# Layer 0's attention scores from float32 to three float32r passes, with the positions on four column tiles and the FFN's sign weights in DRAM

## The chip, the cores and the metric

The kernel runs on one core of a Trainium2 chip. The metric is the device time of one launch in microseconds (us). Kernels are timed in rounds beside the kernel before on the same chip, and nearly all executions agree within 0.3%. A ratio in this text is the mean time of one kernel's fast runs over that of the other's fast runs of the same rounds, so it is not quite the ratio of the medians that stand beside it. The granted clock is the share of its full clock that PE, the engine for matrix products, was given in a stretch.

## The reference

Eight images of 32 x 32 positions with 384 channels go through two layers. Cut to what matters here:

```python
# layer 0 (after a group norm): 6 heads of 64, T = 1024 positions, decomposed relative positions
attn = einsum('bqd,bkd->bqk', q * SCALE, k)
attn = attn + rel_h[:, :, :, :, None] + rel_w[:, :, :, None, :]   # rel_h = q . Rh, rel_w = q . Rw
out  = softmax(attn) @ v;  x = x + (out @ proj_w + proj_b)
# layer 1: causal attention with one head of 384; then, for images 0 to 4 only, an FFN with sign weights
y = quantize(gelu(quantize(ln(x) @ sign(W1 - mean) + b1)) @ sign(W2 - mean) + b2)
```

The scores of layer 0 are by far the largest product: 8 images x 6 heads x 1024 x 1024.

## The kernel before

PE, DVE, ACT and POOL are the engines for matrix products, vector work, activations and general work (GpSimd). SBUF is the memory on the chip that they work on, PSUM the one that PE writes its products to. Column tiles are narrow weights (64 or 32 columns) that stand side by side in PE. Layer 0 handles two heads (a pair `p`, with `par` 0 and 1) at a time. Queries and keys carry the positions in the same 128 rows: 64 rows of q or k, and 64 rows of positions (in `qa`) or of unit rows (in `ka`), so that one float32 product gives q.k plus both position terms.

```python
# POOL: unit rows of ka, 12 copies of 32x1024 for each image                      (L377)
unit = ident[r, r].unsqueeze(2 - d).to_broadcast([32, H, W])
nc.gpsimd.tensor_copy(ka[par][r, p, :].rearrange("i (h w) -> i h w", h=H), unit)
...
# positions: 16 PSUM tiles for each image, 8 small matmuls each, two column tiles  (L402, L403)
nc.tensor.matmul(ps[r0 : r0 + 32, ts(i, 96)], rel[src, 0, win], qv[:, :, at, :], start=True, stop=True)
nc.tensor.matmul(ps[r0 + 32 : r0 + 64, ts(i, 96)], rel[src, 1, win], qv[:, :, :, at], start=True, stop=True)
...   # one DVE copy (L406) and one ACT copy (L409) of each tile into qa
# scores: two float32 matmuls for a 128 x 1024 tile, from a ring of two PSUM tiles (L423, L427)
for half in range(2):
    nc.tensor.matmul(sc[:, half, :], ka[par][:, p, ts(c, P)], qa[par][:, p, ts(half, 512)], start=True, stop=True)
nc.scalar.activation(pr, sc.rearrange("p a n -> p (a n)"), AF.Exp)
...
# P.V: the two heads on two column tiles of 64                                     (L439)
nc.tensor.matmul(avs[half][ts(par, HD), :], v[:, c, ts(h, HD)], prs[par][:, ts(half, 512)], ...)
```

A step `c` of a pair makes the scores of two tiles, then P.V of the step before. There are 3 pairs x 8 steps x 8 images = 192 steps. The order of instructions on each engine is decided when the program is built.

## Time and profile before

| | kernel before |
|---|---|
| time, median | 2955.96 us |
| PE busy | 94% |
| largest group | scores of layer 0, 704 us |
| step of layer 0's attention | 5.50 us |
| prologue (q, k, v, positions) after an FFN / without | 52.8 / 61.0 us |

The profile is read from the bound inwards: the sums say that PE is the bound, the groups say which of its work is largest and that this work waits for nothing, and the timeline gives durations of a stage. The lines themselves are in the prediction below.

### The profile page before, as it was taken

What the parts mean: (1) busy time and instruction counts of PE and PEld (TensorE: products, weight loads), DVE (VectorE), ACT (ScalarE), POOL (GpSimd) and SP (SyncE); (2) the same over time, 40 slices, a digit from 0 to 9 for tenths busy, and PEclk for the clock granted to TensorE, in tenths of its full rate; (3) what the DMA queues carried; (4) which work ended last, traced back from release to release, by engine and by line L of the source; (5) the groups of instructions that cost most, each with busy time, mean ns of one, the idle gap of its engine ahead of it and who ended that gap; (6) DMA issues with size and microseconds to landing.
All of it is one profiled execution on the core that took longest, in us unless ns stands there. A gap on an engine that the chain in (4) does not pass through costs nothing.

```text
span 2952.4 us, 26382 instructions
## 1 busy us (share of the span) xinstructions
PE 2782.4 (94%) x10692; PEld 1460.8 (49%) x10692; DVE 1457.6 (49%) x2402; ACT 929.0 (31%) x1170; POOL 165.4 (6%) x139
## 2 busy tenths in 40 slices
PE   6996989999999999999998999999998999899998
PEld 3433567335664345753457633567434553455345
DVE  3457366453473544744536555357355245523452
ACT  1431154331354312533215432134431143113320
POOL 3000010000020000100001000011001000100000
PEclk9997999999999999999999999999999999999999
DMA  3001001000010000010000100001000100010000
GB/s 108 22 0 64 1 1 65 0 0 1 0 65 1 1 1 0 1 65 0 1 0 1 65 0 1 0 0 65 1 1 0 65 1 0 1 43 1 0 1 23
DMA packets 28066, 49.04 MB, mean 17 GB/s; under 512 B 4256, under 2 KB 24096, under 8 KB 27936
## 3 DMA queue, kind: packets, MB, share of 16 engines
q1 hardware_dynamic: 23648, 43.65, 4.1%
q10 hardware_dynamic: 4288, 3.61, 0.4%
q8 instruction: 86, 1.41, 0.2%
q14 instruction: 44, 0.36, 0.0%
HBM read 34.68 MB, written 12.58 MB: 16 GB/s over the span
## 4 chain that ended last, share of the span: by engine, by line
PE 55%; issue 35%; DVE 5%; ACT 3%; DMA 1%; POOL 0%; ACTq 0%; POOLq 0%; DVEq 0%
PE f_s L423 20%; PE f_av L439 10%; PE f_y L671 6%; PE f_v L329 5%; PE f_qk L319 4%; ACT f_qa L409 3%; PE f_av L569 2%; PE f_s L555 2%; DVE f_h L657 2%; PE f_q L319 2%; PE f_pj L329 1%; PE f_den L451 1%; DVE f_x L680 1%; DVE f_y L679 1%; DMA bv<-in_qkv_b 0%
## 5 line engine op out<-in xcount | busy, mean ns | idle before, releaser
L423 PE MATMUL f_s<-f_qa,f_ka 128*128 128x512 f32 x1536 | 703.9, 603 | 8.3 <-ACT f_qa L409 8.3
L427 ACT ACTIVATE f_pr<-f_s 128x1024 f32<-128x1024 f32 x384 | 393.3, 1024 | 651.4 <-PE f_s L423 651.3
L435 DVE TENSOR_TENSOR f_sum<-f_sum,f_pr 128x1024 f32<-128x1024 f32 x288 | 351.2, 1224 | 344.9 <-ACT f_pr L427 344.3
L423 PEld LDWEIGHTS f_s<-f_qa,f_ka 128*128 128x128 f32 x1536 | 277.9, 189 | 428.0 <-issue 311.2
L439 PE MATMUL f_av<-f_pr,f_v 128*64 128x512 f32 x1536 | 366.6, 603 | 0.0
L319 PE MATMUL f_qk<-f_gnT,wqkv_sb 128*128 128x512 f32 x576 | 254.0, 596 | 2.1 <-DVE f_gnT L278 1.1
L439 PEld LDWEIGHTS f_av<-f_pr,f_v 128*64 128x64 f32 x1536 | 94.3, 136 | 253.5 <-issue 222.6
L671 PE MATMUL f_y<-w2s,f_lo 128*128 128x384 f32 x480 | 172.1, 359 | 34.1 <-DVE f_lo L660 34.1
L569 PE MATMUL f_av<-f_v,f_pr 128*128 128x385 f32 x576 | 194.5, 486 | 0.0
L555 PE MATMUL f_s<-f_q,f_lnT 128*128 128x512 f32 (+3 forms) x576 | 193.8, 486 | 0.0
L319 PEld LDWEIGHTS f_qk<-f_gnT,wqkv_sb 128*128 128x128 f32 x576 | 109.3, 191 | 131.7 <-issue 125.4
L671 PE MATMUL f_y<-w2s,f_hi 128*128 128x384 f32 x480 | 169.5, 353 | 2.7 <-ACT f_hi L658 2.7
L569 PEld LDWEIGHTS f_av<-f_v,f_pr 128*128 128x128 f32 x576 | 108.6, 190 | 78.6 <-issue 11.5
L555 PEld LDWEIGHTS f_s<-f_q,f_lnT 128*128 128x128 f32 x576 | 103.1, 190 | 83.0 <-issue 57.4
L329 PE MATMUL f_pj<-wproj_sb,f_oT 128*128 128x384 f32 x384 | 129.8, 495 | 10.7 <-DVE f_oT L462 10.5
L409 ACT COPY f_qa<-f_rel 32x384 f32<-32x384 f32 x128 | 103.0, 804 | 117.0 <-DVE f_qa L406 114.1
L319 PE MATMUL f_q<-f_lnT,wqk 128*128 128x512 f32 x288 | 136.3, 624 | 0.0
L329 PE MATMUL f_v<-wv_sb,f_lnT 128*128 128x384 f32 x384 | 126.5, 486 | 0.0
L329 PE MATMUL f_v<-wqkv_sb,f_gnT 128*128 128x384 f32 x384 | 126.0, 486 | 0.0
L640 PE MATMUL f_y<-f_lnT,w1s 128*128 128x512 f32 x360 | 118.5, 406 | 5.7 <-ACT f_lnT L301 3.4
L646 DVE TENSOR_REDUCE am<-f_h 128x1 f32<-128x1024 f32 x60 | 73.2, 1220 | 102.0 <-ACT f_h L645 102.0
L454 DVE STREAM_TRANSPOSE f_tr<-f_den 128x512 f32<-128x512 f32 x48 | 34.4, 717 | 168.6 <-PE f_den L451 165.9
(130 smaller groups left out, 2981.9 us busy)
## 6 DMA issues: line engine op xcount, KB each, us to landing
f_gnT<-in_xT SPq DMA_DIRECT2D x24, 512.0 KB, 7.8
f_x<-in_x SPq DMA_DIRECT2D x32, 384.0 KB, 5.1
out_y<-f_x SPq DMA_DIRECT2D x32, 384.0 KB, 2.5
wqkv_sb<-in_qkv_w ACTq DMA_DIRECT2D x1, 1728.0 KB, 10.4
f_w_w<-in_w1T SPq DMA_DIRECT2D x1, 1536.0 KB, 6.2
f_w_w<-in_w2T SPq DMA_DIRECT2D x1, 1536.0 KB, 8.1
f_w_w<-in_w1T SPq DMA_DIRECT2D x1, 768.0 KB, 4.4
f_w_w<-in_w2T SPq DMA_DIRECT2D x1, 768.0 KB, 8.9
```

The lines of the kernel that those rows point to most:

```text
L319: nc.tensor.matmul(ps[:, half, :], w[:, k, cols], xT[:, k, ts(half, 512)], start=(k == 0), stop=(k == NC - 1),)
L329: nc.tensor.matmul(ps[:, :C], xT[:, k, ts(j, P)], w[:, k, cols], start=(k == 0), stop=(k == NC - 1))
L409: nc.scalar.copy(qa[par][rw, :, :].rearrange("k p (h w) -> k p w h", h=H)[:, :, 4 * g : 4 * g + 4, :], pv[rw])
L423: nc.tensor.matmul(sc[:, half, :], ka[par][:, p, ts(c, P)], qa[par][:, p, ts(half, 512)], start=True, stop=True)
L427: nc.scalar.activation(pr, sc.rearrange("p a n -> p (a n)"), AF.Exp)
L435: nc.vector.tensor_tensor(sums[par], prev, prs[par], ALU.add)
L439: nc.tensor.matmul(avs[half][ts(par, HD), :], v[:, c, ts(h, HD)], prs[par][:, ts(half, 512)], start=(c == 0), stop=(c == NJ - 1),)
L555: nc.tensor.matmul(sc[:, half, lo:], xT[:, k, ts(c, P)], q[:, k, half * 512 + lo : (half + 1) * 512], start=(k == 0), stop=(k == NC - 1),)
L569: nc.tensor.matmul(av[:, : C + 1], prs[c][:, ts(j - c, P)], v[:, c, :], start=(c == 0), stop=(c == j))
L640: nc.tensor.matmul(ps[:, half, :], w1s[:, i // 2, ts(m, P)], xs[i % 2][:, i // 2, ts(half, 512)], start=(i == 0), stop=(i == n - 1),)
L646: nc.vector.tensor_reduce(am[:, m : m + 1], h, AX.X, ALU.max, apply_absolute_value=True)
L671: nc.tensor.matmul(ps[:, :C], hs[i][:, m, :], w2s[:, half * 6 + m, :], start=(half == m == i == 0), stop=(half == i == 1 and m == 5),)
```

## The change

The intent is to make the scores cheaper. In the traces a float32 matmul of 512 columns takes two records, about 0.9 us, and a float32r one a single record, 0.2315 us. Each value is split into hi (the value in float32r) and lo (what is left of it). Three float32r products then stand for the float32 one: k(hi,lo) with q(hi,lo) gives two of the terms, the swapped `ks` with q the cross terms, and unit rows with the positions' hi and lo the rest. Everything else follows from that: q must be split before the positions are made, `ks` is copied by POOL, the positions get their own tile `r` with hi and lo, and to make room in SBUF the FFN's sign weights move to DRAM and are loaded for each image with an FFN.

```diff
+            def hi_lo(dst, hi, lo, ps, bias):
+                nc.scalar.activation(dst[hi], ps[hi], AF.Identity, bias=bias[hi])
+                nc.vector.scalar_tensor_tensor(dst[lo], ps[hi], bias[hi], dst[hi].bitcast(F32), ALU.add, ALU.subtract)
 ...
+            def positions(g):        # 4 PSUM tiles for each image, from the scores' ring, four column tiles
+                ps = pools.s_tile(f"rel_{b}_{g}")...
+                            nc.tensor.matmul(ps[ts(2 * par + d, 32), i, :96], rel[:, d, win], ..., start=True, stop=True)
+                for par in range(2):
+                    for d in range(2):
+                        nc.scalar.copy(dst[ts(hi, 32)], src)                                     # L418
+                        nc.vector.tensor_tensor(dst[ts(lo, 32)], src, dst[ts(hi, 32)].bitcast(F32), ALU.subtract)  # L419
 ...
+            for m in range(NPAIR): queries_keys(m)             # q
+            for g in range(4): positions(g)
+            for m in range(NPAIR, 2 * NPAIR): queries_keys(m)  # k, and its swapped copy ks on POOL
+            (v)
 ...
-                for half in range(2):
-                    nc.tensor.matmul(sc[:, half, :], ka[par][:, p, ts(c, P)], qa[par][:, p, ts(half, 512)], start=True, stop=True)
+                for i, (keys, queries) in enumerate(sides[p][par]):     # (k, q), (ks, q), (unit, r)
+                    for half in range(2):
+                        nc.tensor.matmul(sc[:, half, :], keys[:, ts(c, P)], queries[:, ts(half, 512)], start=(i == 0), stop=(i == 2))
 ...
-    w1s = const.tile([P, NC, FF], F32R, name="w1s")
+    w1s = store.tile([P, NC * FF], F32R, name="w1s")            # DRAM; loaded for each FFN by sign_weights(b)
```

The 12 copies of unit rows on POOL for each image are gone with `ka`.

More of the change, by code (lines that the diff above doesn't have):

```diff
@@ L44, in pool @@
             return ctx.enter_context(tc.tile_pool(name=f"{path}_{name}", bufs=bufs, **kw))
-        self.x = pool("x", 1)
-        self.image_ = pool("image", 8)
-        self.page_ = pool("page", 8 if self.fast else 7)
+        self.image_ = pool("image", 11)
+        self.page_ = pool("page", 10 if self.fast else 8)
         self.work = pool("work", 2)
@@ L98, in load_x @@
     def load_x(pools, b):
-        t = pools.x.tile([P, NJ, C], F32, tag="x", name=f"{pools.path}_x_{b}")
+        t = pools.flat(f"x_{b}")[:, : NJ * C].rearrange("p (j c) -> p j c", j=NJ)
         src = x[b].rearrange("(j p) c -> p j c", p=P)
@@ L158, in conv_attn_hybrid @@
     qscale = HD**-0.5
-    bq = const.tile([P, NPAIR], F32, name="bq")
-    nc.vector.tensor_scalar_mul(bq, bqk[:, 0:NPAIR], qscale)
+    nc.vector.tensor_scalar_mul(bqk[:, 0:NPAIR], bqk[:, 0:NPAIR], qscale)
     nc.vector.tensor_scalar_mul(rel, rel, 1.0 / qscale)
+    for k in range(NC):
+        nc.vector.tensor_scalar_mul(wqkv_sb[:, k, 0:C], wqkv_sb[:, k, 0:C], qscale)
+    unit = const.tile([P, T], F32R, name="unit")
+    for i in range(4):
+        r = slice(32 * i, 32 * (i + 1))
+        nc.vector.tensor_copy(
+            unit[r].rearrange("i (h w) -> i h w", h=H), ident[r, r].unsqueeze(2 - i % 2).to_broadcast([32, H, W])
+        )
     N_SEEN = B * (NPAIR + 1)
@@ L178, in judge @@
         nc.vector.tensor_copy(flag, ps[0:1, 0:1])
-    w1s = const.tile([P, NC, FF], F32R, name="w1s")
-    w2s = const.tile([P, NM, C], F32R, name="w2s")
+    store = ctx.enter_context(tc.tile_pool(name="store", bufs=1, space=bass.MemoryType.DRAM))
+    w1s = store.tile([P, NC * FF], F32R, name="w1s")
+    w2s = store.tile([P, NM * C], F32R, name="w2s")
     wqk = const.tile([P, NC, C], F32, name="wqk")
@@ L199, in binarize @@
                 nc.vector.tensor_reduce(part[:, i, g : g + 1], w[:, :, ts(g, gs)], AX.XY, ALU.add)
-            parts.append((w, sign[:, k0:k1, :]))
+            parts.append((w, sign[:, k0 * n_out : k1 * n_out]))
         tot = pools.o_tile(f"tot_{name}")
@@ L205, in binarize @@
         nc.vector.tensor_scalar_mul(mean, tot[:, :NG], 1.0 / (gs * nk * P))
-        for w, s in parts:
+        for i, (w, dst) in enumerate(parts):
+            s = pools.flat(f"sign_{name}_{i}", F32R)[:, : dst.shape[1]].rearrange("p (k o) -> p k o", o=n_out)
             for g in range(NG):
@@ L212, in binarize @@
             nc.vector.scalar_tensor_tensor(s, w, 0.0, s.bitcast(F32), ALU.is_lt, ALU.subtract, reverse1=True)
+            nc.gpsimd.dma_start(out=dst, in_=s.rearrange("p k o -> p (k o)"))
     def multiply_out(pools):
@@ L362, in check, with layer0, queries_keys @@
             nc.vector.tensor_reduce(seen[:, 1, i : i + 1], reciprocal, AX.X, ALU.add)
-        def layer0(xt, b, xT):
-            nc.gpsimd.tensor_tensor(xt, xt, pb.unsqueeze(1).to_broadcast([P, NJ, C]), ALU.add)
-            qa = [pools.image(f"qa_{b}_{par}") for par in range(2)]
-            ka = [pools.image(f"ka_{b}_{par}") for par in range(2)]
-            for p in range(NPAIR):
-                for par in range(2):
-                    r0 = HD * (1 - par)
-                    for d in range(2):
-                        r = slice(r0 + 32 * d, r0 + 32 * (d + 1))
-                        unit = ident[r, r].unsqueeze(2 - d).to_broadcast([32, H, W])
-                        nc.gpsimd.tensor_copy(ka[par][r, p, :].rearrange("i (h w) -> i h w", h=H), unit)
-            lo, hi = slice(0, HD), slice(HD, P)
-            for m in range(2 * NPAIR):
+        def layer0(b, xT):
+            q, k, ks, r = ([pools.image(f"{n}_{b}_{par}", F32R) for par in range(2)] for n in ("q", "k", "ks", "r"))
+            def hi_lo(dst, hi, lo, ps, bias):
+                nc.scalar.activation(dst[hi], ps[hi], AF.Identity, bias=bias[hi])
+                nc.vector.scalar_tensor_tensor(dst[lo], ps[hi], bias[hi], dst[hi].bitcast(F32), ALU.add, ALU.subtract)
+            rows = (slice(0, HD), slice(HD, P))
+            def queries_keys(m):
@@ L380, in layer0 @@
                 p = m % NPAIR
                 ps = project_T(wqkv_sb, ts(m, P), xT, f"qk_{b}_{m}")
-                if m < NPAIR:
-                    nc.vector.tensor_scalar(qa[0][lo, p, :], ps[lo], bqk[lo, m : m + 1], qscale, ALU.add, ALU.mult)
-                    nc.scalar.activation(qa[1][hi, p, :], ps[hi], AF.Identity, bias=bq[hi, m : m + 1], scale=qscale)
-                else:
-                    nc.vector.tensor_scalar(ka[0][lo, p, :], ps[lo], bqk[lo, m : m + 1], None, ALU.add)
-                    nc.scalar.activation(ka[1][hi, p, :], ps[hi], AF.Identity, bias=bqk[hi, m : m + 1])
@@ L388, in layer0 @@
-            v = pools.flat(f"v0_{b}")[:, : NJ * C].rearrange("p (j c) -> p j c", j=NJ)
+                for par in range(2):
+                    hi, lo = rows[par], rows[1 - par]
+                    dst = (q if m < NPAIR else k)[par][:, p, :]
+                    hi_lo(dst, hi, lo, ps, bqk[:, m : m + 1])
+                    if m >= NPAIR:
+                        nc.gpsimd.tensor_copy(ks[par][hi, p, :], dst[lo].bitcast(F32))
+                        nc.gpsimd.tensor_copy(ks[par][lo, p, :], dst[hi].bitcast(F32))
@@ new lines, in positions @@
+            def positions(g):
+                ps = pools.s_tile(f"rel_{b}_{g}").rearrange("p a n -> p (a n)").rearrange("p (i n) -> p i n", i=8)
+                for i in range(8):
+                    at = 8 * g + i
+                    win = slice(H - 1 - at, 2 * H - 1 - at)
+                    for par in range(2):
+                        qv = q[par].bitcast(F32).rearrange("d p (h w) -> d p h w", h=H)
+                        for d in range(2):
+                            nc.tensor.matmul(
+                                ps[ts(2 * par + d, 32), i, :96], rel[:, d, win], qv[:, :, :, at] if d else qv[:, :, at, :],
+                                start=True, stop=True,
+                            )
+                for par in range(2):
+                    for d in range(2):
+                        hi, lo = 2 * par + d, 2 * (1 - par) + d
+                        dst = r[par].rearrange("k p (h w) -> k p w h" if d else "k p (h w) -> k p h w", h=H)[:, :, ts(g, 8), :]
+                        src = ps[ts(hi, 32), :, :96].rearrange("k i (p t) -> k p i t", p=NPAIR)
+                        nc.scalar.copy(dst[ts(hi, 32)], src)
+                        nc.vector.tensor_tensor(dst[ts(lo, 32)], src, dst[ts(hi, 32)].bitcast(F32), ALU.subtract)
@@ L389, in layer0 @@
+            v = pools.flat(f"v0_{b}")[:, : NJ * C].rearrange("p (j c) -> p j c", j=NJ)
+            for m in range(NPAIR):
+                queries_keys(m)
+            for g in range(4):
+                positions(g)
+            for m in range(NPAIR, 2 * NPAIR):
+                queries_keys(m)
             for j in range(NJ):
                 nc.vector.tensor_tensor(v[:, j, :], project(wqkv_sb, slice(2 * C, 3 * C), xT, j, f"v0_{b}_{j}"), bv, ALU.add)
-            for g in range(H // 4):
-                for par in range(2):
-                    src = slice(par * HD, (par + 1) * HD)
-                    r0 = HD * (1 - par)
-                    ps = pools.o_tile(f"rel_{b}_{g}_{par}")
-                    qv = qa[par][src, :, :].rearrange("d p (h w) -> d p h w", h=H)
-                    for i in range(4):
-                        at = 4 * g + i
-                        win = slice(H - 1 - at, 2 * H - 1 - at)
-                        nc.tensor.matmul(ps[r0 : r0 + 32, ts(i, 96)], rel[src, 0, win], qv[:, :, at, :], start=True, stop=True)
-                        nc.tensor.matmul(ps[r0 + 32 : r0 + 64, ts(i, 96)], rel[src, 1, win], qv[:, :, :, at], start=True, stop=True)
-                    rh, rw = slice(r0, r0 + 32), slice(r0 + 32, r0 + 64)
-                    pv = ps[:, :384].rearrange("k (i p t) -> k p i t", i=4, p=NPAIR)
-                    nc.vector.tensor_copy(
-                        qa[par][rh, :, :].rearrange("k p (h w) -> k p h w", h=H)[:, :, 4 * g : 4 * g + 4, :], pv[rh]
-                    )
-                    nc.scalar.copy(
-                        qa[par][rw, :, :].rearrange("k p (h w) -> k p w h", h=H)[:, :, 4 * g : 4 * g + 4, :], pv[rw]
-                    )
@@ L413, in layer0 @@
-            (attend0_fast if pools.fast else attend0_general)(xt, b, qa, ka, v)
-        def attend0_fast(xt, b, qa, ka, v):
+            xt = load_x(pools, b)
+            nc.gpsimd.tensor_tensor(xt, xt, pb.unsqueeze(1).to_broadcast([P, NJ, C]), ALU.add)
+            sides = [[[(t[par][:, p, :], u[par][:, p, :]) for t, u in ((k, q), (ks, q))] + [(unit, r[par][:, p, :])]
+                      for par in range(2)] for p in range(NPAIR)]
+            (attend0_fast if pools.fast else attend0_general)(xt, b, sides, v)
@@ L418, in attend0_fast @@
+            return xt
+        def attend0_fast(xt, b, sides, v):
             oT = pools.image(f"oT_{b}")
@@ L421, in scores @@
                 sc = pools.s_tile(f"s0_{b}_{p}_{c}_{par}")
-                for half in range(2):
-                    nc.tensor.matmul(
-                        sc[:, half, :], ka[par][:, p, ts(c, P)], qa[par][:, p, ts(half, 512)], start=True, stop=True
-                    )
+                for i, (keys, queries) in enumerate(sides[p][par]):
+                    for half in range(2):
+                        nc.tensor.matmul(
+                            sc[:, half, :], keys[:, ts(c, P)], queries[:, ts(half, 512)], start=(i == 0), stop=(i == 2)
+                        )
                 pr = pools.page(f"pr0_{b}_{p}_{c}_{par}")
@@ L486, in attend0_fast, with attend0_general @@
                 nc.vector.tensor_tensor(xt[:, j, :], project(wproj_sb, slice(0, C), oT, j, f"pj_{b}_{j}"), xt[:, j, :], ALU.add)
-        def attend0_general(xt, b, qa, ka, v):
+        def attend0_general(xt, b, sides, v):
             state = {}
@@ L496, in scores @@
                 sc = pools.s_tile(f"s0_{b}_{j}_{h}")
-                for half in range(2):
-                    nc.tensor.matmul(
-                        sc[:, half, :], qa[par][:, p, ts(j, P)], ka[par][:, p, ts(half, 512)], start=True, stop=True
-                    )
+                for i, (keys, queries) in enumerate(sides[p][par]):
+                    for half in range(2):
+                        nc.tensor.matmul(
+                            sc[:, half, :], queries[:, ts(j, P)], keys[:, ts(half, 512)], start=(i == 0), stop=(i == 2)
+                        )
                 return softmax_numerator(
@@ L629, in absmax_scale, with sign_weights @@
             return s, up, low
+        def sign_weights(b):
+            half = 3 * T // 2
+            a1, a2, rest = (pools.flat(f"{n}_{b}", F32R)[:, : 3 * T] for n in ("w1a", "w2a", "wrest"))
+            nc.gpsimd.dma_start(out=a1, in_=w1s[:, : 2 * half])
+            nc.gpsimd.dma_start(out=rest[:, :half], in_=w1s[:, 2 * half :])
+            nc.gpsimd.dma_start(out=a2, in_=w2s[:, : 2 * half])
+            nc.gpsimd.dma_start(out=rest[:, half:], in_=w2s[:, 2 * half :])
+            w1k = [a1[:, ts(i, FF)] for i in range(2)] + [rest[:, :FF]]
+            w2m = [a2[:, ts(i, C)] for i in range(8)] + [rest[:, half + i * C : half + (i + 1) * C] for i in range(4)]
+            return w1k, w2m
         def ffn(xt, b):
@@ L633, in ffn @@
             quarters = [pools.image(f"h{i}_{b}") for i in range(4)]
+            w1k, w2m = sign_weights(b)
             am = pools.small.tile([P, NM], F32, tag="am", name=f"am_{b}")
@@ L640, in ffn @@
                         nc.tensor.matmul(
-                            ps[:, half, :], w1s[:, i // 2, ts(m, P)], xs[i % 2][:, i // 2, ts(half, 512)],
+                            ps[:, half, :], w1k[i // 2][:, ts(m, P)], xs[i % 2][:, i // 2, ts(half, 512)],
                             start=(i == 0), stop=(i == n - 1),
@@ L671, in ffn @@
                             nc.tensor.matmul(
-                                ps[:, :C], hs[i][:, m, :], w2s[:, half * 6 + m, :],
+                                ps[:, :C], hs[i][:, m, :], w2m[half * 6 + m],
                                 start=(half == m == i == 0), stop=(half == i == 1 and m == 5),
@@ L684, in run @@
             for b in range(B):
-                xt = load_x(pools, b)
-                layer0(xt, b, gn)
+                xt = layer0(b, gn)
                 if pools.fast and b == 0:
```

## The prediction

> **What bounds the kernel now.** I read the page first: its sums, the chain that ended last, the costliest groups.
>
> ```profile
> PE 2782.4 (94%) x10692; PEld 1460.8 (49%) x10692; DVE 1457.6 (49%) x2402; ACT 929.0 (31%) x1170; POOL 165.4 (6%) x139
> ...
> PE f_s L423 20%; PE f_av L439 10%; PE f_y L671 6%; PE f_v L329 5%; PE f_qk L319 4%; ACT f_qa L409 3%; PE f_av L569 2%; PE f_s L555 2%; DVE f_h L657 2%; PE f_q L319 2%; PE f_pj L329 1%; PE f_den L451 1%; DVE f_x L680 1%; DVE f_y L679 1%; DMA bv<-in_qkv_b 0%
> ...
> L423 PE MATMUL f_s<-f_qa,f_ka 128*128 128x512 f32 x1536 | 703.9, 603 | 8.3 <-ACT f_qa L409 8.3
> L427 ACT ACTIVATE f_pr<-f_s 128x1024 f32<-128x1024 f32 x384 | 393.3, 1024 | 651.4 <-PE f_s L423 651.3
> L435 DVE TENSOR_TENSOR f_sum<-f_sum,f_pr 128x1024 f32<-128x1024 f32 x288 | 351.2, 1224 | 344.9 <-ACT f_pr L427 344.3
> ...
> L409 ACT COPY f_qa<-f_rel 32x384 f32<-32x384 f32 x128 | 103.0, 804 | 117.0 <-DVE f_qa L406 114.1
> ...
> L406 DVE COPY f_qa<-f_rel 32x384 f32<-32x384 f32 x128 | 70.5, 550 | 37.6 <-PE f_rel L403 34.8
> ```
>
> TensorE is the bound, busy 94% of a 2952.4 us span. Its largest group is layer 0's scores (L423), 704 us, which wait for nothing but 8.3 us at their starts. ACT's exponentials and DVE's sums wait for PE, not the other way round. One stage is different: the relative positions (f_rel), where ACT waits for DVE and the chain runs through ACT's copy L409 (3%).
>
> Next I read the timeline of PE in attention 0 of image 1, and in FFN layer 1 of image 0:
>
> ```profile
> 525.94 3.70 PE L423 MATMUL f_s<-f_qa,f_ka 128*128 128x512 f32 x8
> 529.57 1.94 PE L439 MATMUL f_av<-f_pr,f_v 128*64 128x512 f32 x8
> 531.44 3.70 PE L423 MATMUL f_s<-f_qa,f_ka 128*128 128x512 f32 x8
> ```
> ```profile
> 379.77 0.62 PE L640 MATMUL f_y<-f_lnT,w1s 128*128 128x512 f32 x2
> ...
> 385.79 0.62 PE L640 MATMUL f_y<-f_lnT,w1s 128*128 128x512 f32 x2
> ```
>
> Scores start 5.50 us apart (525.94 to 531.44): 3.63 us for two score tiles, 1.87 us for P·V. Eight records make four float32 matmuls of 512 columns (two records each), so one takes 3.63/4 = 0.907 us. The FFN's float32r matmuls of the same size, one record each, come 26 in 6.02 us between the two rows shown: 0.2315 us each.
>
> Last, sums of engines by stretch: score stage of an image with FFN beside it, score stage without, and the prologues (q, k, v, positions) without and after an FFN:
>
> ```profile
> 517.04:909.61 392.57, 374.61 (x1468) 206.39 (x1469) 205.95 (x350) 136.34 (x180) 20.16 (x16) 0.97 0.04 13
> 2396.78:2705.11 308.33, 298.33 (x1109) 139.71 (x1109) 129.57 (x196) 81.63 (x92) 20.37 (x14) 0.98 0.03 11
> 2335.82:2396.78 60.96, 59.90 (x377) 34.56 (x376) 21.97 (x35) 18.83 (x22) 6.68 (x1) 1.00 0.16 59
> 464.20:517.04 52.84, 51.59 (x358) 30.66 (x356) 28.49 (x53) 17.69 (x21) 7.02 (x2) 1.00 0.25 90
> ```
>
> After the stretch's length come busy times of PE, PEld, DVE, ACT, POOL, then the granted clock. PE is nearly always full, so PE time removed in the score stage should come off the end, and a pause put into a prologue should be added to it.
>
> **What the Trainium skill says.** "FP8 and Floating Point Precision", TensorE Precision Notes: FP32 is done in four passes over high and low parts, and the quicker mode truncates to FP22. The trace agrees on the pace (0.907/0.2315 = 3.9), and this is why the change carries hi and lo parts and three products. "TensorEngine Tiling (Array Packing)", PSUM Bottleneck: once TensorE is packed, the copies out of PSUM may become the limit. The positions stage already agrees: 8 matmuls on two column tiles end in 0.67 us, while ACT's L409 needs 0.80 per tile. "TensorE: Matmul & The Clock Gate", Part 1: idle windows bring the clock down. Here, after a PE gap of 6.81 us at 420.6, the granted clock over 427–440 was 0.78.
>
> **The change part by part.**
>
> 1. Scores. Per score tile, 2 float32 matmuls (1.815 us) become 3 passes × 2 halves = 6 × 0.2315 = 1.39 us. Per pair and column: 12 × 0.2315 = 2.78 instead of 3.63, −0.85. There are 1536 records/8 = 192 such steps: **−163 us**. The new step is 2.78 + 1.87 = 4.65 us. It leaves room for ACT (2 × 1.02) and DVE (at most 2 × 1.22). Two score buffers suffice, as an exponential (1.02 us) fits into the other tile's 1.39.
>
> 2. Prologue. q must now be split before the positions, which read hi and lo stacked; k and v come after. So the built order is q, (v0–v3 pulled forward), positions 0–3, k, the rest of v, scores. q, k, positions and scores share one ring of two PSUM tiles: positions 2 and 3 wait until 0 and 1 are emptied, and k's first two until 2 and 3 are. PE has little to do meanwhile. On one PSUM tile ACT and DVE take turns, as they do now (L384 has 156.3 us idle until DVE L383; L409 has 114.1 until L406). Each of the 4 positions tiles takes four ACT copies of 32x768 and four DVE subtractions, ACT first. L409 gives ACT at stride 1.67 ns an element plus about 0.16 us, so 1.45 us strided; unstrided about 0.80 (estimate, half the slope). DVE's L302 (128x384 from PSUM, 557 ns) gives 0.95 us unstrided; strided lies somewhere in 0.95–1.75 (estimate). ACT: 4 × 4 copies, half of each kind, 18.0 us. I laid these out by hand in the built order, two tiles interleaved: from the first positions matmul to k's first, 22.5 us with DVE at full rate, 25 in the middle, 28.4 at its worst; 14.6 now (2382.13 to 2396.78). I use 24.5, thus +9.9.
>    After an FFN: y2 ends at 464.2 and DVE's tail lasts until 475.3, so q's last tile is split late and positions begin about 14.9 us after y2. Then 24.5, k's last 15.8 and v's 7.7, and about 1.7 for the clock after the pauses: 64.6 against 52.8, **+11.8 × 5 = +59**. Without FFN (two images): 73 against 61.0, **+24**. Image 0: +12, less 5 because the early POOL copies that stretched the `rel` scaling to 6.69 us go: **+7**. Together **+90**.
>
> 3. End of layer 0. The next image's load (3 × 512 KB, 7.8 us to landing) now takes a slot that the last scores read (k); before, it had been done in mid-attention. Its six statistics (0.67 us each) stand in DVE's order around the transposition of the last denominators, before the output projection, which has 10.5 us of waiting on DVE already. Estimate +2 × 7 = **+14 us**, at worst 6 × 7.
>
> 4. Image 0's binarizing. The reductions of w2 (6.2 us) and the next image's statistics (about 5) now stand behind w1's signs on DVE, which the gate mean waits for; PE has 19.8 us idle there already. **+13 us**, a rough estimate.
>
> 5. Sign weights from DRAM: 4.7 MB for each FFN image. The loads start when layer 0's v, oT and q buffers come free, some 90 us ahead of FFN layer 1 and 40 us ahead of layer 2; 1536 KB took 6.2–8.1 us. Hidden, 0. POOL's 12 copies an image (each about 1.1 us) replace as many for ka, and x's later load is hidden too.
>
> Sum: −163 + 90 + 14 + 13 = −46; 2955.96 − 46 = **2910 us** (−1.6%).
>
> **The rivals.**
>
> (a) The positions cost less: the matmuls of four column tiles and the evacuations interleave better, the strided subtractions run at DVE's unstrided pace, the DVE tail is pulled forward. For it: the engines' own work (18 us of ACT) is only 3.4 above today's 14.6. Against: the turns, 156.3 and 114.1 us of idle time already. With +4 an image instead of about +11, and parts 3 and 4 at half: 2955.96 − 163 + 32 + 14 = 2839; with one of the two, 2870–2890.
>
> (b) Float32r passes in attention don't reach the FFN's pace. If a matmul took 3.63/12 = 0.30 us, nothing would be gained and the time would be about 3070. Against: in the FFN every matmul has new weights, here two share one; ACT and DVE have spare time. At 0.25 us: 12 × 0.0185 × 192 = 43 us less gain, 2953.
>
> (c) The sign weights arrive late. Then FFN layer 1 would start after a DMA wait of about 10 us, ×5: 2960. Against: the buffers' release times and the DMA queues are nearly idle (the page's DMA row has 1 tenth at most after the start).
>
> (d) The exponential takes over as the limit of the score stage, since the two-buffer ring lets the scores run only one tile ahead: 0.1–0.2 us per tile × 384 = 38–77 us, so 2950–2990. For it: 1.39 against 1.02 plus a start-up of some 0.2 is little slack; against: P·V lies between every other pair of tiles.
>
> **Range and chances.** The first term is firm: its pace is measured in this very trace. The loss is not: the prologues may cost +30 to +125, parts 3 and 4 +5 to +55. Both extremes together give 2828 and 2973; they will hardly meet, (b) to (d) only push up, and (a) is the likeliest miss. I take 2850 to 2975. Faster by 2% means below 2896.8, 13 us under my number: 0.38. Slower by 2% means above 3015, which needs (b) or (c) as well: 0.06. The rest is 0.56.
>
> **What would show it.** The changed profile should show score matmuls 1.39 us per tile and steps 4.65 us apart; PE in layer 0's prologue idle some 5–8 us twice while ACT and DVE take turns on f_rel, from its first matmul to k's 22–28 us; FFN prologues of 62–67 us; the projection of layer 0 starting 2 us later after the last P·V; a PE gap in image 0 of over 30 us before FFN layer 1; no DMA releasing FFN matmuls. I am wrong if the score step is not 4.65, or if the positions stage stays near 14.6 us, or if PE waits for sign weights.

## The result

The changed kernel took 2926.36 us (median of 4 runs, 2921.59 to 2929.08) against 2955.22 us for the kernel before in the same rounds: ratio 0.9900 (95% interval 0.9883 to 0.9917), 1% faster and inside the 2% that counts as the same. The time lies 16 us above the predicted 2910 and within the range. As will be seen, this is a sum of larger errors of both signs.

The page of the changed kernel, the lines that answer to those of before:

```profile
PE 2675.7 (91%) x11460; PEld 1585.1 (54%) x11460; DVE 1570.0 (54%) x2457; ACT 1019.7 (35%) x1218; POOL 193.6 (7%) x163
...
L447 PE MATMUL f_s<-f_q,f_k 128*128 128x512 f32 x768 | 260.0, 420 | 0.0
L447 PE MATMUL f_s<-f_q,f_ks 128*128 128x512 f32 x768 | 240.9, 394 | 0.0
L447 PE MATMUL f_s<-f_r,unit 128*128 128x512 f32 x768 | 240.8, 395 | 0.0
...
L419 DVE TENSOR_TENSOR f_r<-f_rel,f_r 32x768 fp32r<-32x768 f32 x128 | 153.3, 1197 | 93.0 <-ACT f_r L418 90.8
...
L418 ACT CAST f_r<-f_rel 32x768 fp32r<-32x768 f32 x128 | 143.7, 1123 | 101.2 <-DVE f_r L419 52.5
```

The scores' 1536 float32 records (703.9 us) are now three groups of 768, one for each product, at about 0.4 us a record instead of 0.6. Those means overlap, because matmuls are pipelined, so they are no pace. PE is down from 2782 to 2676 us busy and from 94 to 91%: there are pauses now. The copies of positions have turned from 103.0 + 70.5 us of ACT and DVE into 143.7 + 153.3, each waiting for the other.

To see where the time went I cut both traces at the first and last records of each stage on PE and added the stages over the images:

| stage (us, summed over its images) | before | changed | difference | predicted |
|---|---|---|---|---|
| start to image 0's first score | 92.8 | 101.8 | +9.0 | +7 |
| scores of layer 0, first to last | 1049.8 | 927.8 | −122.0 | −163 |
| projection, with the wait for it | 182.9 | 191.3 | +8.4 | +14 |
| image 0, projection to end of attention 1 | 118.1 | 130.3 | +12.2 | +13 |
| attention 1 of the others, norm, FFN layer 1 | 853.0 | 853.3 | +0.3 | 0 |
| FFN layer 1's end to layer 2's end, five images | 261.9 | 230.7 | −31.2 | 0 |
| prologue after an FFN, five images | 264.2 | 335.3 | +71.1 | +59 |
| prologue without FFN, two images | 121.9 | 147.1 | +25.2 | +24 |
| end | 8.0 | 9.5 | +1.5 | 0 |
| span | 2952.4 | 2927.0 | −25.4 | −46 |

Two rows stand out: the scores gained 41 us less than predicted, and FFN layer 2 gained 31 us that nobody had predicted.

**The scores.** The timeline of PE in image 3, changed kernel (start, duration, line, count of records):

```profile
1314.70 0.73 PE L447 MATMUL f_s<-f_q,f_k 128*128 128x512 f32 x2
1315.26 0.62 PE L447 MATMUL f_s<-f_q,f_ks 128*128 128x512 f32 x2
1315.72 0.63 PE L447 MATMUL f_s<-f_r,unit 128*128 128x512 f32 x2
...
1317.11 0.63 PE L447 MATMUL f_s<-f_r,unit 128*128 128x512 f32 x2
1317.67 1.94 PE L463 MATMUL f_av<-f_pr,f_v 128*64 128x512 f32 x8
1319.54 0.73 PE L447 MATMUL f_s<-f_q,f_k 128*128 128x512 f32 x2
```

Steps are 4.84 us apart (1314.70 to 1319.54), not 4.65. Inside the block the pairs of records start 0.46 us apart (1315.26 to 1315.72), which is the pace of 0.2315 that the prediction took from the FFN. But the first pair takes 0.56 (1314.70 to 1315.26), and so does the last one before P.V (1317.11 to 1317.67). Looking at single records of both traces, the same excess is in the kernel before:

| from start to start, us | before | changed |
|---|---|---|
| two score records inside a block | 0.428 | 0.2315 |
| last score record to first P.V record | 0.523 | 0.329 |
| first pair of P.V records to the second (0.429 between later ones) | 0.480 | 0.480 |
| last pair of P.V records to first score record | 0.522 | 0.523 |
| first score record to the second | 0.534 | 0.336 |

Against the pace inside the blocks the last four intervals cost 0.095 + 0.051 + 0.093 + 0.106 = 0.35 us a step before, and 0.35 us after. The score weights fill 128 columns, those of P.V 64, on two column tiles. The float32 pace itself can be read where no such change occurs, in the q and k projections of the kernel before:

```profile
464.05 12.18 PE L319 MATMUL f_qk<-f_gnT,wqkv_sb 128*128 128x512 f32 x28
```

28 records in 12.18 us, less the 0.59 that the last one is drawn long, give 11.59/27 = 0.429 us a record, 0.86 for a matmul of 512 columns, not 0.907. So the pace that the prediction had read off the block of scores (3.63/4) was the matmuls plus the change.

**FFN layer 2.** Its start in image 3 of the kernel before, all engines:

```profile
1592.65 13.17 POOL L377 COPY f_ka<-ident 32x1024 f32<-32x1024 f32 x12
...
1593.25 10.45 DVE L657 TENSOR_SCALAR f_h<-f_h,qu,ql 128x384 f32<-128x384 f32 x10
...
1604.98 0.69 PE L671 MATMUL f_y<-w2s,f_lo 128*128 128x384 f32 x1 [6.82 <-DVE f_lo L660]
```

and in the changed kernel:

```profile
1586.47 4.57 DVE L695 TENSOR_SCALAR f_h<-f_h,qu,ql 128x384 f32<-128x384 f32 x10
...
1591.55 0.44 PE L709 MATMUL f_y<-f_w2a,f_lo 128*128 128x384 f32 x1 [0.34 <-DVE f_lo L698]
```

Ten clamps on DVE took 10.45 us beside POOL's copies of the next image's unit rows and 4.57 us without them, and PE's pause before layer 2 fell from 6.82 us to 0.34. The prediction had quoted the same pause of image 0 (6.81 us), but only as evidence on the clock.

**The prologue.** Two stretches of the changed kernel, in the columns of the prediction: positions of image 3, and a prologue after an FFN:

```profile
1257.00:1281.00 24.00, 8.88 (x192) 7.42 (x189) 16.82 (x15) 16.44 (x15) 0.00 (x0) 0.69 0.09 32
1628.70:1696.10 67.40, 50.77 (x354) 28.37 (x352) 43.66 (x56) 28.50 (x26) 8.64 (x9) 0.87 0.14 47
```

In the 24 us of positions 1 to 3 PE is busy for 8.88 us, ACT for 16.44 and DVE for 16.82, and the granted clock is 0.69. From the first record of the positions to k's first it takes 29 us (1252.1 to 1281.0), where the prediction had 24.5 and 28.4 as the worst. Two lines of PE from image 4's prologue:

```profile
1670.28 18.51 PE L330 MATMUL f_qk<-f_gnT,wqkv_sb 128*128 128x512 f32 x36 [6.46 <-DVE f_r L419]
1688.62 7.90 PE L340 MATMUL f_v<-wqkv_sb,f_gnT 128*128 128x384 f32 x24
```

k's three projections, 15.8 us in the prediction, take 18.3 (1670.28 to 1688.62) after a pause of 6.46.

### The profile page after: what moved, and what is told of

Read it like the earlier page. It is cut to its first block, busy times and chain, and to the rows that moved or that the text cites. A ratio compares the mean times of both kernels' runs of the same rounds, so it can differ in the third digit from the quotient of the medians.

```text
span 2927.0 us, 28173 instructions
## 1 busy us (share of the span) xinstructions
PE 2675.7 (91%) x11460; PEld 1585.1 (54%) x11460; DVE 1570.0 (54%) x2457; ACT 1019.7 (35%) x1218; POOL 193.6 (7%) x163
## 4 chain that ended last, share of the span: by engine, by line
PE 75%; DVE 13%; ACT 3%; issue 1%; POOL 0%; POOLq 0%; DVEq 0%; ACTq 0%
PE f_s L447 17%; PE f_av L463 10%; PE f_v L340 6%; PE f_av L594 6%; PE f_s L580 6%; PE f_y L678 6%; PE f_qk L330 6%; PE f_y L709 5%; PE f_q L330 5%; PE f_pj L340 4%; DVE f_r L419 3%; ACT f_r L418 2%; PE f_pt L244 2%; DVE f_h L695 1%; PE f_den L475 1%
## 5 line engine op out<-in xcount | busy, mean ns | idle before, releaser
L330 PE MATMUL f_qk<-f_gnT,wqkv_sb 128*128 128x512 f32 x576 | 278.0, 636 | 52.9 <-DVE f_r L419 51.8
L447 PE MATMUL f_s<-f_q,f_k 128*128 128x512 f32 x768 | 260.0, 420 | 0.0
L447 PE MATMUL f_s<-f_q,f_ks 128*128 128x512 f32 x768 | 240.9, 394 | 0.0
L447 PE MATMUL f_s<-f_r,unit 128*128 128x512 f32 x768 | 240.8, 395 | 0.0
L447 PEld LDWEIGHTS f_s<-f_q,f_k 128*128 128x128 f32 x768 | 128.6, 188 | 154.5 <-ACT f_pr L451 110.0
L419 DVE TENSOR_TENSOR f_r<-f_rel,f_r 32x768 fp32r<-32x768 f32 x128 | 153.3, 1197 | 93.0 <-ACT f_r L418 90.8
L418 ACT CAST f_r<-f_rel 32x768 fp32r<-32x768 f32 x128 | 143.7, 1123 | 101.2 <-DVE f_r L419 52.5
L447 PEld LDWEIGHTS f_s<-f_r,unit 128*128 128x128 f32 x768 | 144.2, 188 | 34.4
L447 PEld LDWEIGHTS f_s<-f_q,f_ks 128*128 128x128 f32 x768 | 144.2, 188 | 34.2
L409 PE MATMUL f_rel<-f_q,rel 128*32 128x96 f32 x2048 | 95.8, 316 | 68.7 <-DVE f_r L419 61.2
L340 PE MATMUL f_pj<-wproj_sb,f_oT 128*128 128x384 f32 x384 | 133.2, 505 | 15.7 <-DVE f_oT L486 14.8
## 6 DMA issues: line engine op xcount, KB each, us to landing
wqkv_sb<-in_qkv_w ACTq DMA_DIRECT2D x1, 1728.0 KB, 10.7
```

What stands on the lines that cost most here:

```text
L330: nc.tensor.matmul(ps[:, half, :], w[:, k, cols], xT[:, k, ts(half, 512)], start=(k == 0), stop=(k == NC - 1),)
L340: nc.tensor.matmul(ps[:, :C], xT[:, k, ts(j, P)], w[:, k, cols], start=(k == 0), stop=(k == NC - 1))
L418: nc.scalar.copy(dst[ts(hi, 32)], src)
L419: nc.vector.tensor_tensor(dst[ts(lo, 32)], src, dst[ts(hi, 32)].bitcast(F32), ALU.subtract)
L447: nc.tensor.matmul(sc[:, half, :], keys[:, ts(c, P)], queries[:, ts(half, 512)], start=(i == 0), stop=(i == 2))
```

## The experiments

Theory: the cost of changing column tiling ate a quarter of the gain that had been expected of the scores; POOL's copies had cost the kernel before about 6 us an image; the taking of turns on the positions and PE's pauses make the prologue's loss. The main rivals are named with each run. All runs gave a result that the comparison with the reference accepts. The comparison also accepts wide_av and f32_scores, which are wrong, so it says nothing about the precision of the three passes. The changed kernel was timed only beside the result, not again in the rounds of these runs (on chips 3, 14 and 4); the kernel before was, and its medians agree (2955.0 to 2955.8 us). "Under" or "over the changed kernel" therefore compares across rounds.

### pairs: half as many changes between scores and P.V

```diff
-                pending = None
+                pending = []
 ...
-                    if pending:
-                        values(p, *pending, sums, avs)
-                    pending = (c, prs)
+                    if c % 2:
+                        for u in pending: values(p, *u, sums, avs)
+                        pending = []
+                    pending.append((c, prs))
```

> Changed kernel, but two steps of scores are issued before two steps of P.V, so that PE changes between 128-column score weights and 64-column P.V weights 4 times for a pair of heads and not 7. Theory: each change costs 0.1 us in each direction (seen in both traces: 0.52 instead of 0.43 us between the last score record and the first P.V record), whatever the number format. Then 3 x 0.2 us x 24 = 14 us less than the changed kernel: about 2912 us, and the records inside a block of scores stay 0.23 us apart. Rival: the extra 0.2 us of a step are a slower pace of the float32r passes themselves, so no change, 2926. Second rival: the two score buffers hold the scores up behind the exponential; then four score tiles in a row must be slower, over 2930, with PE idle behind ACT's exponential.

Measured: 2885.68 us, ratio to before 0.9771 (0.9758 to 0.9784), 41 us under the changed kernel. PE in image 3:

```profile
1303.76 0.63 PE L447 MATMUL f_s<-f_r,unit 128*128 128x512 f32 x2
1304.32 3.65 PE L463 MATMUL f_av<-f_pr,f_v 128*64 128x512 f32 x16
1307.91 0.73 PE L447 MATMUL f_s<-f_q,f_k 128*128 128x512 f32 x2
1308.48 0.63 PE L447 MATMUL f_s<-f_q,f_ks 128*128 128x512 f32 x2
```

Now 16 records of P.V run at once; the change is still there once for each block (1303.76 to 1304.32 and 1307.91 to 1308.48 are 0.56 and 0.57 us for pairs of records). Eight steps of a pair of heads take 39.4 us instead of 40.4. That is three changes of 0.35 us, so 1.05 and not the 0.6 that I had expected, because I had counted two of the four intervals of the table. Over 24 pairs of heads it is 24 us, which is what the scores and the wait behind them lost together (−37.3 + 13.2; one more P.V now stands at the end). Both rivals fall: the pace inside the blocks is unchanged, and four score tiles in a row don't wait for the exponential. The other 17 us are not due to this: the projections shrink by 6.5 us as the last P.V gives the next image's statistics time, and the start, attention 1 and the norms lose some 12 more, which I did not trace further.

### wide_av: the same number formats, no change of tiling

```diff
-                            avs[half][ts(par, HD), :], v[:, c, ts(h, HD)], prs[par][:, ts(half, 512)],
+                            avs[half], v[:, c, ts(p, P)], prs[par][:, ts(half, 512)],
 ...   # and start and stop, for two products into one tile
```

> Changed kernel, P.V with 128-column weights (both heads' V) and without column tiles, still float32: four matmuls one after the other, a wrong result on purpose. Theory (the cost of a change belongs to the change between 128 and 64 columns, not to that between float32r and float32): a step is 12 x 0.2315 + 4 x 0.856 = 6.20 us, and the interval from the last score record to the first P.V record is 0.23 us. Rival (the number format changes): 6.20 + 0.35 = 6.55 us, the interval 0.33 us.

Measured, in one execution of unknown state, of which only the trace's intervals are used: 3194.22 us, as P.V does twice the work. The output is wrong by construction. Steps are 6.23 us apart, where the theory said 6.20 and the rival 6.55. PE at one change:

```profile
1502.24 0.62 PE L447 MATMUL f_s<-f_r,unit 128*128 128x512 f32 x2
1502.70 7.03 PE L463 MATMUL f_av<-f_pr,f_v 128*128 128x512 f32 x16
```

From float32r scores to float32 P.V the interval of two records is 0.46 us (1502.24 to 1502.70), as inside the block, where the changed kernel has 0.56. Single records give the same on the way back: from the last record of P.V to the second of the scores it is 0.66 us, which is 0.43 + 0.23. So the cost belongs to the change between 128 columns and two column tiles of 64, and not to that of the number format.

### f32_scores: the scores alone put back to float32

```diff
-                for i, (keys, queries) in enumerate(sides[p][par]):
+                for keys, queries in sides[p][par][:1]:
 ...
-                            sc[:, half, :], keys[:, ts(c, P)], queries[:, ts(half, 512)], start=(i == 0), stop=(i == 2)
+                            sc[:, half, :], keys[:, ts(c, P)].bitcast(F32), queries[:, ts(half, 512)].bitcast(F32), start=True, stop=True
```

> Changed kernel, but each score tile again in one float32 product of two 512-column matmuls (of k and q hi alone with the lo rows, without positions: a wrong result on purpose; everything else stays). Theory: inside a block a float32 matmul takes 0.856 us and a float32r pass 0.2315, so the three passes saved 4 x 0.856 - 12 x 0.2315 = 0.65 us a step and 124 us in all: 2926 + 124 = 3050, steps of 5.50 us. What the rest of the change costs is then 3050 - 2955 = 95 us. Rival (the prediction's 0.85 us a step holds and other parts of the score stage took 40 us away): 3089.

The output is wrong by construction here too, as the positions are left out. Measured: 3040.74 us, ratio 1.0287 (1.0271 to 1.0302); steps of 5.50 us; the scores' stage is 1049.1 us, as in the kernel before. So the three passes are worth 121 us in that stage and 114 us in the whole (the projections were 10 us shorter here), and all the rest of the change costs 3040.7 − 2955.8 = 85 us. The rival, 3089 us, falls.

### dummy: POOL copies put back beside FFN layer 2

```diff
+            nc.vector.tensor_scalar(ident3, ident, low, None, ALU.mult)
+            for i in range(32):
+                nc.gpsimd.tensor_copy(spare[r]..., ident3[...].to_broadcast([32, 12, W]))
```

> Changed kernel with 32 useless GpSimd copies (32x384, as many elements as the removed 12 copies of 32x1024) placed where the kernel before ran its copies of unit rows: right after the scale of FFN layer 1, beside the clamps of layer 2 on DVE. Theory: these copies slowed DVE's first ten clamps from 4.6 to 10.5 us and with them the start of layer 2; putting such copies back costs 5 to 6 us in each of five images: 2926 + 28 = about 2954, with the clamps at about 1 us each again. Rival: layer 2 got shorter because its order of instructions changed: then 2926 to 2930, clamps at 0.46.

Measured: 2948.17 us, ratio 0.9974 (0.9961 to 0.9987), 22 us over the changed kernel. FFN layer 2 took 258.5 us in the five images instead of 230.7, so 5.6 us an image came back. Second products of layer 2 (name, shape, count, busy time, mean, idle time before and its releaser), changed kernel and this run:

```profile
L709 PE MATMUL f_y<-f_w2a,f_lo 128*128 128x384 f32 x320 | 115.2, 360 | 2.4 <-DVE f_lo L698 1.9
```

```profile
L719 PE MATMUL f_y<-f_w2a,f_lo 128*128 128x384 f32 x320 | 115.6, 361 | 23.2 <-DVE f_lo L708 23.1
```

PE waits for DVE's subtraction again, 23.2 us instead of 2.4; before it was 34.1. One detail missed: the ten clamps took 5.51 us, not 10; the clamps were slowed less, but these copies last longer (18.1 us an image, about 13 before), and DVE's later subtractions were slowed as well (629 ns in the mean after 549). The rival, another order of instructions, falls.

### ka_late: the kernel before, its POOL copies after the FFN

```diff
+            nc.vector.scalar_tensor_tensor(ident2, xt[:, NJ - 1, 0:P], 0.0, ident, ALU.mult, ALU.add)   # at the FFN's end
-                        unit = ident[r, r].unsqueeze(2 - d)...
+                        unit = ident2[r, r].unsqueeze(2 - d)...
```

> Kernel before, its GpSimd copies of unit rows made to wait until the FFN of the previous image has ended (they read a copy of the identity that DVE writes from the FFN's last output tile). Theory: the gap of 6.8 us before FFN layer 2 goes, 5 x 6 = 30 us less than the kernel before: about 2925; some of it may come back where the copies now run beside DVE in the prologue, so 2925 to 2940. Rival (not the copies): 2955.

Measured: 2950.23 us, ratio 0.9977 (0.9963 to 0.9991): only 5 us less. In the trace FFN layer 2 became 42.7 us shorter (261.9 to 219.2), more than expected, but the prologues after an FFN became 26.4 longer and the scores 8.4. DVE's instructions there are no slower; PE pauses for some 4 us in such a prologue (57.40 us long, 53.15 busy, clock 0.94), and q, k and v had been put in another order by the build. So the place of the loss is confirmed (the stage shrank once the copies were gone from it), but this run doesn't say what removing the copies would be worth alone. I expected 2925 to 2940 and was wrong.

### split: ACT's copies first, then DVE's subtractions

```diff
-                        nc.scalar.copy(dst[ts(hi, 32)], src)
-                        nc.vector.tensor_tensor(dst[ts(lo, 32)], src, dst[ts(hi, 32)].bitcast(F32), ALU.subtract)
+                        sides_.append((dst[ts(hi, 32)], dst[ts(lo, 32)], src))
+                for h, _, src in sides_: nc.scalar.copy(h, src)
+                for h, l, src in sides_: nc.vector.tensor_tensor(l, src, h.bitcast(F32), ALU.subtract)
```

> Changed kernel, but of each tile of relative positions first the four ACT copies, then the four DVE subtractions, so ACT and DVE take turns twice for a tile and not eight times. Theory: the turns cost the positions stage its pauses (ACT's 18 us and DVE's 19 us of work take 27 us); with half overlap the stage loses about 2.5 us, 8 x 2.5 = 20 us: about 2906. Rival: DVE needs ACT's result anyway, and now the first subtraction waits for four copies: no change or up to 2 us an image slower, 2926 to 2942.

Measured: 2908.7 us, ratio 0.9840 (0.9827 to 0.9853), 18 us under the changed kernel. The copies' own line:

```profile
L421 ACT CAST f_r<-f_rel 32x768 fp32r<-32x768 f32 x128 | 143.8, 1124 | 76.4 <-PE f_rel L409 64.5 <-DVE f_r L423 10.4
```

ACT's waits fell from 101.2 to 76.4 us, those for DVE from 52.5 to 10.4; the durations stayed. The prologues became 9.4 us shorter after FFNs and 1.4 without, the start 4.7. So the turns cost something, but less in the prologues than I had expected (11 of 20 us).

### split_v: part of v into the pause

```diff
-            for g in range(4): positions(g)
-            (k, then v)
+            positions(0); positions(1)
+            (v)
+            positions(2); positions(3)
+            (k)
```

> As split, and v4 to v7 are issued between positions 1 and 2 instead of after k. Theory: PE waits there (8.7 us in a profiled image) for the two PSUM tiles to be emptied by ACT and DVE; the 7.9 us of v then cost nothing, less the 2.2 us that their additions take from DVE among the subtractions: 5 to 6 us an image after an FFN, less in the other three, so 35 us under split (2908.7): about 2874. Rival: the additions of v push every later subtraction back, so under 10 us is left: 2900.

Measured: 2913.4 us, ratio 0.9855 (0.9840 to 0.9870): no gain over split. Both halves of the theory can be seen in the trace, and they cancel. Against split, the prologues became 22.7 us shorter after FFNs and 8.9 without, as expected. But the scores' stage grew from 927.8 to 964.9 us, nearly all in its first step (6.3 to 8.8 us instead of 3.1). ACT at that place of image 3:

```profile
1289.68 1.11 ACT L384 ACTIVATE f_k<-f_qk,bqk 64x1024 fp32r<-64x1024 f32 x1 [1.75 <-PE f_qk L330]
1290.81 1.28 ACT L457 ACT_TABLE_LOAD   x1
1292.11 1.02 ACT L457 ACTIVATE f_pr<-f_s 128x1024 f32<-128x1024 f32 x1
1293.16 1.11 ACT L384 ACTIVATE f_k<-f_qk,bqk 64x1024 fp32r<-64x1024 f32 x1
```

With nothing after k, the first exponential, with its table load of 1.28 us, gets between the two halves of k's last evacuation on ACT. PE shows what it waits for there:

```profile
1293.18 1.22 PE L453 MATMUL f_s<-f_q,f_k 128*128 128x512 f32 x2 [2.14 <-ACT f_pr L457]
...
1296.04 2.14 PE L469 MATMUL f_av<-f_pr,f_v 128*64 128x512 f32 x4
...
1301.11 1.93 PE L469 MATMUL f_av<-f_pr,f_v 128*64 128x512 f32 x4
...
1305.97 1.94 PE L469 MATMUL f_av<-f_pr,f_v 128*64 128x512 f32 x8
```

The second score tile waits 2.14 us for the first one's exponential; that k's last product still holds the other tile of the ring fits, but no run shows it. And the first step's P.V now comes in two lots of four records, one head each: a lot takes as long (1.9 us) as eight records do when both column tiles run. Together that is 4.0 us, about the growth in the images whose first step is 7.2 us. In image 3 the scores after the pause are slower besides (0.43 us a record, granted clock 0.71 over 1291 to 1296). In the two images that follow an image without FFN the first step is 6.3 us; there the wait is 1.11 us, without a table load. This was in neither of my theories.

### gn_late: the next group norm after attention 1

```diff
-                gn = group_norm_T(b + 1) if b + 1 < B else None
                 attention1(xt, b)
+                gn = group_norm_T(b + 1) if b + 1 < B else None
```

> Changed kernel, the next image's group norm emitted after attention 1, so its statistics no longer stand before the last denominators and projections on DVE. Theory (part 3 of the prediction): the projection goes back from 17.8 to 19.7 us to 17.2 in every image, about 10 us in all, and image 0 gains some of the statistics' 5 us: 2910 to 2917. Rival: the statistics were not what lengthened the projection: 2926; or the prologue of the next image now starts late: over 2930.

Measured: 2908.9 us, ratio 0.9839 (0.9826 to 0.9853), 17 us under the changed kernel. The projections went back to 138.3 us in all (changed kernel 148.0, before 140.4), and image 0 became 14.8 us shorter up to the end of attention 1 (115.5 instead of 130.3). The projections agree with the theory; image 0 gained more than it said, because attention 1 no longer waits there for the group norm. In the two images without FFN attention 1 became 12.5 us shorter and the next prologue 15.6 longer, so there the next image does start late, as the rival had it.

### twice: the sign weights loaded twice

```diff
             (four loads of w1s and w2s)
+            (the same four loads again)
```

> Changed kernel, each image's sign weights loaded from DRAM twice, one load after the other into the same tiles. Theory (part 5 of the prediction): the loads end long before the FFN asks for them, so doubling them costs nothing: 2926, within 6 us. Rival: the loads are in the way of something (DMA queues, GpSimd's issuing, the slots): 10 us or more.

Measured: 2914.93 us, ratio 0.9858 (0.9843 to 0.9873). Doubling the loads costs nothing. That it was 11 us lower than the changed kernel in other rounds I can't explain: the stages differ by 1 or 2 us in several places with no pattern (projections of 18.0 or 19.7 us in different images). Differences of 10 us between single variants are therefore not to be leaned on without the trace.

### mix1, mix4, mix3: putting the gains together

mix1 is pairs, split_v and gn_late. 

> pairs, split_v and gn_late together. If the three parts lie at different places of an image and add up: 2926.4 - 40.7 (pairs) - 17.7 (split) - 35 (v) = 2833, a little less with gn_late, of which pairs already had a part. Rival: they overlap (the projection is gained twice, the prologue's pauses once), 2850 to 2870.

Measured: 2892.19 us, ratio 0.9775 (0.9758 to 0.9792), no better than pairs alone (0.9771). Two of its five executions took 2880 us and three 2892 to 2894; I don't know why, and the trace is of a 2880. The scores' stage is 38.0 us longer than in pairs, with the long first step of split_v (7.2 to 8.8 us), and the prologues without FFN 5.4 us longer; gn_late had the same.

mix4 is pairs and split, with the late group norm for image 0 alone. 

> pairs and split together, and the next group norm after attention 1 for image 0 alone (in images without FFN it lengthened the prologue). v stays after k. If they add up: 2885.7 - 17.7 - 10 = 2858. Rival: as in mix1, gains overlap, 2870 to 2885.

Measured: 2868.27 us, ratio 0.9700 (0.9686 to 0.9713); 10 us short of the plain sum.

mix3 adds a cure for split_v's long first step:

```diff
+            positions(0); positions(1)
+            (v0 to v5 here: v4 and v5 fall between positions 1 and 2)
+            positions(2); positions(3)
+            (k)
+            both = pools.s_tile(f"v0_{b}_67")     # v6 and v7, in the scores' PSUM ring, so after k
```

> mix4, and v4 and v5 between positions 1 and 2, v6 and v7 in the PSUM ring of the scores after k. Theory from split_v and mix1: v between the positions shortens the prologue by as much PE time as it moves, but with nothing after k the scores wait 4 to 6 us for k's last hi and lo; two tiles of v (3.9 us) after k cover most of that wait. Then 3.9 us less an image than mix4: 8 x 3.9 = 31, so 2827, and the first step of the scores is about 3.1 us again, not 7.2. Rival: the scores wait for k's last evacuation all the same: no gain over mix4.

Measured: 2847.12 us, ratio to before 0.9629 (0.9616 to 0.9642). PE at the beginning of image 3's scores:

```profile
1262.41 2.10 PE L442 MATMUL f_v<-wqkv_sb,f_gnT 128*128 128x384 f32 x6
1265.67 2.20 PE L442 MATMUL f_v<-wqkv_sb,f_gnT 128*128 128x384 f32 x6 [1.17 <-DVE f_v L446]
1267.64 0.71 PE L464 MATMUL f_s<-f_q,f_k 128*128 128x512 f32 x2
```

v6 and v7 stand after k with a wait of 1.17 us, and the scores then run without one; their first step is 2.87 us. mix3 beats both kernels: 3.7% under the kernel before and 79 us under the changed one. It gained 21 us over mix4, not the 31 expected.

## Why the prediction was right or wrong

The total was right within its range; the composition was not.

1. **Scores: mechanism right, term mis-sized.** The step that failed is "Eight records make four float32 matmuls of 512 columns (two records each), so one takes 3.63/4 = 0.907 us". It divides the time of a whole block, with the change of tiling at its edges, by the number of matmuls. The pace inside is 0.856, and the 0.35 us of the change stay in the new step: 4 x 0.856 − 12 x 0.2315 = 0.65 us saved, not 0.85, so 124 us and not 163. The trace shows 122, f32_scores 121. By its own sign, "I am wrong if the score step is not 4.65", the prediction was wrong here: the step is 4.85. The Trainium skill had the clue, "TensorEngine Tiling (Array Packing)", Key Properties: "Changing tiling mode (not just tile) drains the TensorE". I had read the page for its other section only. Traces agree that the change costs time, and pairs and wide_av show how much; that it is a drain, no run here shows.

2. **Prologue: right in kind, a little short after FFNs.** Without FFN +25.2 instead of +24; after FFNs +71.1 instead of +59. Of the terms, DVE's strided subtraction was 1.44 us (inside the guessed 0.95–1.75) and ACT's copies 0.79 and 1.45 (0.80 and 1.45 estimated). What failed is the choice "I use 24.5": it was 29 us. Which part of it was short stays open. Measured is that a tile's 32 matmuls take 2.5 to 3.0 us from first to last record (4.6 or more in an image's first tile), no faster for each than on two column tiles (0.67 us for 8). k then ran at a lowered clock (0.85), 18.3 us. That the positions began sooner after layer 2 (12.6 us instead of 14.9) gave part of it back. Of the 96 us of this loss, split took back 11 and mix3, which contains it, 27, by fewer turns and filled pauses; that the rest consists of these too is read from the trace (PE is busy 8.88 of 24 us) and not shown by a run.

3. **End of layer 0: right in kind, somewhat smaller.** +8.4 us instead of +14. In the seven images that were meant it is +10.7, and gn_late takes exactly that back; image 0 lost 2.3 us there, because the reductions of w2 had left its projection (see 4).

4. **Image 0: right, in size and in its parts.** +12.2 instead of +13. In the kernel before, DVE made the reductions of w2 and the next image's statistics beside the projection (before 248.3 us). In the changed kernel both stand where the prediction put them, in DVE's order behind w1's signs (which end at 258.9):

```profile
258.85 5.43 DVE L208 TENSOR_REDUCE part_w<-f_w_w 128x1 f32<-128x608 f32 x10
...
276.56 1.28 DVE L257 BATCH_NORM_STATS2 gst<-f_gnT 128x6 f32<-128x512 f32 x2
```

   The reductions take 5.43 us (6.2 predicted), and the statistics, to 280.87, 4.3 (about 5). gn_late gains 14.8 us here by another way: the reductions stay where they are, but attention 1 no longer waits for the group norm at all.

5. **Sign weights: right, except for one sentence.** The loads are hidden, as twice shows. But "POOL's 12 copies an image (each about 1.1 us) replace as many for ka, and x's later load is hidden too" was wrong as an account of zero. The copies for ka were not hidden: beside FFN layer 2 they slowed DVE, on which PE waited. FFN layer 2 became 31 us shorter without them, and dummy puts 28 us of it back in the same place. That these 31 us nearly made up for the 41 missing from the scores, so that the total came out right, is luck. No instruction of PE waits for the new copies of ks in the trace, so for them the sentence holds.

Of the rivals, (b) comes nearest in size: its line "At 0.25 us: 12 x 0.0185 x 192 = 43 us less gain" meets the missing 41 us, but by another mechanism, as the passes do reach the FFN's pace. (c) and (d) did not occur. (a) did not either.

What remains open: the precision of the three passes, what POOL's copies are worth in the kernel before by themselves (ka_late changed the order of q, k and v too), and the 11 us by which twice lies under the changed kernel, which was not timed again in those rounds.

## What to carry to other kernels

Read a pace between the starts of neighbouring records inside a run, never as a block's time over its count: a fixed cost at the edges looks like work, and it stays when the work gets faster. When a change removes work from an engine off the critical path, ask which pauses of the bound engine lay beside that work; here this was worth a quarter of the main gain. Work that fills a pause should not be the work that hid another wait: moving all of v cost what it gained, and leaving its last two tiles after k (mix3) kept part of the gain.

## What the Trainium skill lacked or had wrong

- "TensorEngine Tiling (Array Packing)", Key Properties, names the drain when the tiling mode changes but no cost: here 0.35 us for going from 128 columns to two tiles of 64 and back, seven times for each of 24 pairs of heads (59 us); issuing two steps together took 24 us of it away.
- The same page counts four parallel column tiles of 32. Small float32 products of 96 columns gained nothing from them here: 32 matmuls on four took 2.5 us at best, 8 on two took 0.67, so 0.08 us each in both. A tile of positions took 2.90 us at a granted clock of 0.50 (1267.7 in the changed kernel) and 2.88 at 1.00 (495.4), so something other than that clock set this pace. What it was is open, and the page is not shown to be wrong.
- "GPSIMD Engine Reference", Specifications, says that GpSimd shares SBUF access with VectorE; that section gives no size. Ten DVE clamps of 128x384 took 10.45 us beside copies of 32x1024 and 4.57 without.
- "PSUM — Partial Sum Buffer", PSUM bank collisions raise a hardware error, says that two engines may use different quadrants of a bank at the same time. In the kernel before, ACT still took its half of a tile of q only after DVE had ended with the other (L384 after L383, 24 times, 1.27 us of DVE each); no run here tried to lift it, so this is a point about the build and not about the page.
